# A two-layer perceiver on one Trainium2 core: the first layer's job order, its zero fills, one maximum over partitions and one projection's instruction order

## The chip, the cores and the metric

The kernel runs on one core of one Trainium2 chip. The metric is the device time of an execution in microseconds, given as the median of three runs. One further execution was profiled; the rows quoted below come from it. Engines are named as in the profile: PE (matrix multiply), DVE (vector), ACT (scalar, activation functions), POOL (general purpose), SP (issues most DMA transfers). Each engine takes its own instructions in order, and waits for others by semaphores.

## What is computed

The input x is 64 sequences of 32 tokens of width 256 (2048 tokens), beside a context of 64 x 257 x 256. Two layers follow, each with cross-attention, self-attention and a feed-forward block, all added to x after a layer norm. Everything is float32. Layer 0's blocks, cut to what matters here:

```
x = x + xattn(layernorm(x), ctx)             # 16 heads, causal: token l sees ctx[0..l]
x = x + attn(layernorm(x)) * gate ...        # 16 heads, position bias, tanh gate
# feed-forward with quantization to 16 bits ("qdq"):
def act_qdq(x):
    scale = maximum(max(abs(x)) / 32767, 1e-12)      # one maximum over the whole tensor
    return clip(round(x / scale), -32768, 32767) * scale
x = act_qdq(x); up = act_qdq(x @ deq(w_up).T); gate = act_qdq(x @ deq(w_gate).T)
sig = fixed_qdq_u16(sigmoid(gate)); gate = act_qdq(gate * sig); o = act_qdq(gate * up)
out = o @ deq(w_down).T
```

The three feed-forward weights are themselves rounded to 4 bits in blocks of 32 (`deq`).

## The kernel before

**Jobs.** Cross-attention and self-attention of layer 0 are cut into 16 jobs of 256 tokens (two tiles of 128): the order is x0 to x4, then a0, x5, a1, x6, a2, x7, then a3 to a7, where x is a cross-attention job and a a self-attention job. A loop over t = 0..15 (line 719 on) is a software pipeline written out by hand: in step t, job t is projected (values, keys, queries, L215 and L396), job t-1 gets its scores, maxima and exponentials (L255/L265, L282, L287, L697), job t-2 its normalization and block transposition (`weights_job`, L291 to L302) and its spread over four batch masks by ACT (L311), job t-3 its weighted sums (L322) and, at the end of its way, output projection (L347). A self-attention job that is done gives, in step t+4, the transposed input of the feed-forward block and its maximum (`f0_input`). Inside `tc.manual_schedule` the instructions of PE, DVE, ACT and POOL stand in the order in which they are written; SP's DMA issues are placed by the scheduler.

**Beside the jobs** the loop spreads other work: `dequantize` is a generator with 19 steps, one `next` each. For each of three weights: a DMA load, a maximum by block and its reciprocal (L508 to L511), multiplication and rounding (L513, L514), multiplication by the scale (L516), then three groups of four PE transposes with an ACT copy (L524, L527). `bias_heads` (L598) makes the position bias, `lines_matrices` (L423 to L455) small matrices for layer 1.

**Layer norm.** Statistics by DVE (L160, L161), rstd by two POOL instructions (L163, L164), the normalization xn by DVE (L368), then POOL adds a bias row to x (L414).

**Zeros.** `value_tiles` fills the tiles vz of the values with zeros once, by POOL (L481); the values are then written into every other block.

**The maximum over partitions** is `scale_of`/`scale_steps`: DVE reduces over the free axis (L537), POOL's `partition_all_reduce` over the partitions (L539). It is called for the quantized input ("x"), the gate, up, and two products. After step 1 of the loop there is one more such call on a constant, `warm` (L767).

**Gate projection.** 12 chunks of 1024 tokens by 128 features: four matmuls (L966), a copy by ACT (L971), a maximum by DVE (L359). In the same loop layer 1's weights are read chunk by chunk into two buffers (wck, L846) and OR-ed into `lost_bits` by DVE (L853). This loop is not in a hand-written order: the scheduler interleaves.

Of the kernel before, what the change touches and what calls it, by code (L numbers as in the profile page):

```python
# [11 lines left out]
F32 = mybir.dt.float32  # L12
# [4 lines left out]
ALU = mybir.AluOpType  # L17
AX = mybir.AxisListType
# [5 lines left out]
P = 128  # L24
# [42 lines left out]
def tile_perceiver(ctx: ExitStack, tc: tile.TileContext, d: dict, out: bass.AP):  # L67
    nc = tc.nc
# [26 lines left out]
    def load_x(n):  # L95
        nc.sync.dma_start(x[:, 2 * n : 2 * n + 2, :], x_view[:, 2 * n : 2 * n + 2, :])
# [10 lines left out]
    def load_rows(queue, a, b):  # L107
        queue.dma_start(
            rows[:, a:b].rearrange("p r e -> p (r e)"), d["rows"][a * D : b * D].partition_broadcast(P)
        )  # L110

    load_rows(nc.scalar, 0, 2)
    ident = const.tile([P, P], F32, tag="ident", name="ident")
    make_identity(nc, ident)
    eps = const.tile([P, 1], F32, tag="eps", name="eps")
    nc.gpsimd.memset(eps, EPS)
    mhalf = const.tile([P, 1], F32, tag="mhalf", name="mhalf")
    nc.gpsimd.memset(mhalf, -0.5)
    magic = const.tile([P, 1], F32, tag="magic", name="magic")
# [30 lines left out]
    def load_w(pool, name, n, kt=2):  # L150
        w = pool.tile([P, kt, n], F32, tag=name, name=name)
        nc.sync.dma_start(w, d[name].rearrange("(k p) n -> p k n", p=P))
        return w
# [49 lines left out]
    def row2(pool, name):  # L203

        r2 = pool.tile([P, 2, D], F32, tag=f"r_{name}", name="row2", bufs=1)
        nc.gpsimd.tensor_copy(r2, bc(row(name), 1, 2))
        return r2
# [265 lines left out]
            if i == 0:  # L473
                yield

    def value_tiles(pool, n):

        vzs = []
        for i in range(n):
            vz = pool.tile([P, 2, 8, 3, HD], F32, tag=f"vz{i}", name=f"vz{i}", bufs=1)  # L480
            nc.gpsimd.memset(vz, 0.0)  # L481
            vzs.append(vz)
        return cycle(vzs)

# [41 lines left out]
                    )  # L526
                nc.scalar.copy(flat[:, n0 * P : (n0 + 4) * P], pt)  # L527

    def scale_of(mx, tag, pre=None):
        *_, sr = scale_steps(mx, tag, pre)  # L530
        return sr

    def scale_steps(mx, tag, pre=None):


        m1 = small.tile([P, 1], F32, tag="m1", name="m1")
        nc.vector.tensor_reduce(m1, mx, AX.X, ALU.max)  # L537
        m2 = small.tile([P, 1], F32, tag="m2", name="m2")
        nc.gpsimd.partition_all_reduce(m2, m1, P, bass_isa.ReduceOp.max)  # L539
        yield  # L540
        s = small.tile([P, 1], F32, tag=f"s{tag}", name="s", bufs=1)
        if pre is not None:
            nc.vector.tensor_tensor(m2, m2, pre, ALU.mult)
        nc.vector.tensor_scalar(s, m2, 1.0 / QMAX, 1e-12, ALU.mult, ALU.max)
        r = small.tile([P, 1], F32, tag=f"r{tag}", name="r", bufs=1)
        nc.vector.reciprocal(r, s)
        if pre is not None:
            nc.vector.tensor_tensor(r, r, pre, ALU.mult)
        yield s, r


    with (
# [15 lines left out]
        x0_wv = load_w(wp, "x0_wv", D)  # L568
        x0_wk = load_w(wp, "x0_wk", D)
        x0_wq = load_w(wp, "x0_wq", D)  # L570
        load_x(1)
        load_c(1)
        x0_wo = load_w(wp, "x0_wo", D)
# [40 lines left out]
        def norm_job(w):  # L614
            w["xns"] = normalized(pool, w["n"], w["stats"])
            add_row2(w["n"], "a0_bo" if w["a"] else "x0_bo")

        def inputs_job(w):
            w["xT"] = pool.tile([P, 2, 2 * P], F32, tag="xT", name="xT", bufs=2)
            transposed(w["xns"], w["xT"])  # L620
# [15 lines left out]
        def keys_products(w):  # L636
            if w["a"]:
                w["pk"] = proj2(a0_wqkv, D, w["xT"])
            else:
                w["pk"] = proj2(x0_wk, 0, cTs[w["n"]])  # L640
                load_c(w["n"] + 3)

        def keys_apart(w):


            kb = w["kb"] = pool.tile([P, 2, 8, 4, L], F32, tag="kb", name="kb", bufs=2)
            bh = bias_of_head["a0_bk" if w["a"] else "x0_bk"]
            for m in range(2):
                for h in range(4):
                    nc.scalar.activation(  # L650
                        kb[:, m, :, h, :], w["pk"][:, m].rearrange("p (b l) -> p b l", l=L),
                        AF.Identity, bias=bh[:, m, h : h + 1], scale=h4[:, h : h + 1],
                    )
# [60 lines left out]


        with tc.manual_schedule(engines=hand_order):
            vzs = value_tiles(pool, 4)
            r2_x0 = row2(pool, "x0_bv")
            stats_of_job(jobs[0])
            norm_job(jobs[0])  # L720
            for t in range(NJ):
                proj, soft, turn, sums, done = (job(t - k) for k in range(5))
                f0 = done is not None and done["a"]
                if t < 2:
                    values_job(proj)
                    keys_products(proj)
                if turn:
                    weights_job(turn)
                if f0:
                    f0_input(done, 0)  # L730
                if job(t + 1):
                    stats_of_job(job(t + 1))
                if sums:
                    sums_job(sums)
                if f0:
                    f0_input(done, 1)
                if soft:
                    scores_job(soft)
                inputs_job(proj)
                if sums and proj["a"]:  # L740
                    out_job(sums)
                if t >= 2:
                    values_job(proj)
                if soft:
                    shift_job(soft)
                if turn:
                    spread_job(turn)
                if f0:
                    f0_input(done, 2)
                if soft:  # L750
                    exp_job(soft)
                if job(t + 1):
                    norm_job(job(t + 1))
                queries_job(proj)
                if t >= 2:
                    keys_products(proj)
                keys_apart(proj)
                gate_job(proj)
                if sums and not proj["a"]:
                    out_job(sums)  # L760
                if t == 0:
                    nc.vector.tensor_copy(mask8, bc(causal, 1, 8))
                elif t == 1:
                    r2_a0 = row2(pool, "a0_bv")

                    warm = small.tile([P, 1], F32, tag="m2", name="warm")
                    nc.gpsimd.partition_all_reduce(warm, eps, P, bass_isa.ReduceOp.max)  # L767
                elif t == 2:
                    bias_heads()
                    lines_of = lines_matrices(pool)  # L770
                elif t in (5, 6, 7):
                    next(lines_of, None)
                for _ in range(2 if 1 <= t <= 3 else 1):
                    next(dequantizing, None)
            for _ in dequantizing:
                pass


            j12, j13, j14, j15 = jobs[NJ - 4 :]
            weights_job(j14)  # L780
            sums_job(j13)
            scores_job(j15)
            shift_job(j15)
            spread_job(j14, 0, 2)
            exp_job(j15)
            spread_job(j14, 2, 4)
            out_job(j13)
            f0_input(j12, 0)
            weights_job(j15)
            f0_input(j12, 1)  # L790
            spread_job(j15, 0, 4, dve=(1, 3))
            sums_job(j14)
            f0_input(j12, 2)
            f0_input(j13, 0)
            sums_job(j15)
            f0_input(j13, 1)
            out_job(j14)
            f0_input(j13, 2)
            f0_input(j14, 0)
            out_job(j15)  # L800
            f0_input(j15, 0)
            f0_input(j14, 1)
            f0_input(j15, 1)
            f0_input(j14, 2)
            f0_input(j15, 2)


            sx, rx = scale_of(f0_mx, "x")
            for st in range(NST):
                xs = f0_xT[:, st].rearrange("p k n -> p (k n)")  # L810
                if st % 2 == 0:
                    nc.vector.tensor_scalar(xs, xs, rx, MAGIC, ALU.mult, ALU.add)
                else:
                    nc.scalar.activation(xs, xs, AF.Identity, bias=magic, scale=rx)
                nc.vector.tensor_scalar(xs, xs, MAGIC, sx, ALU.subtract, ALU.mult)
# [136 lines left out]
    with tc.tile_pool(name="f0", bufs=1, reuse_waits="tile") as pool:  # L952
# [19 lines left out]
            absmax(mx[:, c : c + 1], pm)  # L972

        mx = small.tile([P, NC], F32, tag="mx_g", name="mx", bufs=1)
        for c in range(NC):
            project(wgtT, g, c, mx)
            or_bits(weights_of(wck_pool, "wck", 2, *chunks[c]))
        checkp.close()
        sigp = ExitStack()
        sig_pool = sigp.enter_context(tc.tile_pool(name="sig", bufs=1, side="right", reuse_waits="tile"))  # L980
# [191 lines left out]
    with tc.tile_pool(name="x1", bufs=1, reuse_waits="tile") as pool:  # L1172
# [198 lines left out]
            load_ctx()  # L1371


        vzs = value_tiles(pool, 2)
        NP = 2 * H
        NP2 = NTILE // 2
        lns = []
# [597 lines left out]
```

## Time and profile before

| what | us |
|---|---|
| median of three runs (lowest, highest) | 1340.51 (1339.69, 1340.77) |
| the profiled execution's own time | 1338.12 |
| its span, first to last instruction | 1336.3 |
| layer 0's 16 jobs, first PE work to the maximum m (L537) | 8.28 to 256.48 |
| gate and up projections on PE begin (L966) | 262.76 |
| PE busy | 1227.4 |
| DVE busy | 908.6 |
| ACT busy | 719.7 |
| POOL busy | 159.9 |

A row of the timeline gives start, duration, engine, line, operation, and in brackets how long the engine was idle before it and what released it; "issue" stands for a wait for nothing that the profile shows. The chain of waits goes back from the last instruction, at each step to what released it. Rows of stretches give the busy time of every engine in a window.

### The profile page before, as it was taken

The numbers are of one execution on the slowest core, as the hardware profiler recorded it, in microseconds if no ns is written. First come the engines' busy times: TensorE is split into PE (matmuls) and PEld (weight loads), VectorE is DVE, ScalarE is ACT, GpSimd is POOL, SyncE is SP. The second block draws the span as 40 slices with busy tenths as digits, with TensorE's granted clock in tenths as the row PEclk, the third lists the DMA queues.
The fourth block names the chain that finished last, engine by engine and source line by source line (L and its number), as shares of the span: only waits on it lengthen the run. The fifth ranks groups of instructions, "written<-read, shape, count | busy, mean of one in ns | idle before, by whom it ended". The sixth has DMA issues, their size and how long they took to land.

```text
span 1336.3 us, 28421 instructions
## 1 busy us (share of the span) xinstructions
PE 1227.4 (92%) x11694; PEld 955.4 (72%) x11694; DVE 908.6 (68%) x1781; ACT 719.7 (54%) x1515; POOL 159.9 (12%) x423
## 2 busy tenths in 40 slices
PE   5799989599869999999999999999769999999998
PEld 4687878344558777777777777777557888888887
DVE  4788887866993488768787887777667363453633
ACT  3688878237693355667676766666535321131311
POOL 3111120100001012221212121211100000000000
PEclk9899999799989999999999999999879999999999
DMA  9200100230131342112111111110015100000000
GB/s 244 43 9 3 57 26 14 75 131 0 56 118 40 108 128 72 42 53 57 46 53 45 46 45 51 32 29 2 2 36 202 50 16 1 16 1 0 17 0 18
DMA packets 63127, 66.31 MB, mean 50 GB/s; under 512 B 21072, under 2 KB 52624, under 8 KB 62992
## 3 DMA queue, kind: packets, MB, share of 16 engines
q1 hardware_dynamic: 62416, 63.93, 16.1%
q8 instruction: 94, 1.54, 0.5%
q10 hardware_dynamic: 576, 0.50, 0.2%
q14 instruction: 41, 0.34, 0.1%
HBM read 57.53 MB, written 6.89 MB: 48 GB/s over the span
## 4 chain that ended last, share of the span: by engine, by line
PE 64%; DVE 23%; ACT 7%; issue 3%; DMA 2%; POOL 1%; SPq 0%; DVEq 0%; ACTq 0%; POOLq 0%
PE mm L1779 21%; PE mm L396 5%; PE mm L884 5%; PE mm L895 4%; PE pp L966 3%; PE mm L1274 3%; PE o L1112 3%; PE mm L215 3%; DVE nm L1236 2%; DVE mx L359 2%; PE s L1225 2%; PE o L1846 2%; DVE pe L1255 2%; PE o L1294 2%; PE o L347 1%
## 5 line engine op out<-in xcount | busy, mean ns | idle before, releaser
L1779 PE MATMUL mm<-hl,f_h 128*128 128x512 f32 x1024 | 232.9, 389 | 1.1 <-ACT sl L1824 1.1
L1779 PEld LDWEIGHTS mm<-hl,f_h 128*128 128x128 f32 x1024 | 192.2, 188 | 41.2 <-issue 1.4
L884 PE MATMUL mm<-ct,x_wk 128*128 128x257 f32 x512 | 132.2, 402 | 14.9 <-ACT kb L890 13.7
L1243 ACT ACTIVATE pe<-s,nm 128x257 f32<-128x257 f32 x256 | 118.2, 482 | 45.9 <-DVE nm L1236 21.1
L1837 ACT ACTIVATE g<-mm,cols 128x512 f32<-128x512 f32 x64 | 44.0, 688 | 164.8 <-PE mm L1779 163.6
L1785 DVE CAST hl<-g 128x512 fp32r<-128x512 f32 x64 | 27.3, 427 | 147.5 <-ACT g L1837 147.5
L895 PE MATMUL mm<-x_wv,ct 128*128 128x256 f32 x512 | 121.1, 379 | 0.4 <-ACT vb L929 0.4
L884 PEld LDWEIGHTS mm<-ct,x_wk 128*128 128x128 f32 x512 | 95.3, 196 | 36.6 <-ACT kb L890 15.7
L895 PEld LDWEIGHTS mm<-x_wv,ct 128*128 128x128 f32 x512 | 97.0, 190 | 14.6 <-ACT vb L929 0.8
L311 ACT ACTIVATE pb<-pt,masks 128x1024 f32<-128x1024 f32 x90 | 96.8, 1142 | 16.9 <-DVE pt L302 16.9
L1236 DVE TENSOR_REDUCE nm<-s 128x4 f32<-128x1028 f32 x64 | 78.2, 1222 | 15.1 <-PE s L1225 15.1
L890 ACT ACTIVATE kb<-mm,cols 128x257 f32<-128x257 f32 x128 | 57.7, 476 | 53.6 <-PE mm L884 49.8
L1263 POOL TENSOR_TENSOR px<-pe,rec 32x4 f32<-32x4 f32 x256 | 50.9, 199 | 276.5 <-DVE rec L1253 232.3
L1255 DVE TENSOR_SCALAR pe<-pe,rec 128x256 f32<-128x256 f32 x256 | 78.9, 371 | 5.4
L1274 PE MATMUL mm<-ident,pe 128*128 128x128 f32 x512 | 76.1, 283 | 7.0 <-DVE pe L1255 4.5
L1274 PEld LDWEIGHTS mm<-ident,pe 128*128 128x128 f32 x512 | 60.2, 142 | 23.6 <-issue 6.1
L414 POOL TENSOR_TENSOR x<-x,rows 128x512 f32<-128x512 f32 x32 | 45.3, 1415 | 133.9 <-DVE xn L368 130.7
L1243 ACT ACTIVATION_READ_ACCUMULATOR pe<-s,nm 128x1 f32 x256 | 54.9, 214 | 0.0
L911 DVE COPY vb<-mm 128x512 f32<-128x512 f32 x55 | 37.7, 685 | 23.9 <-PE mm L895 21.3
L384 ACT COPY xT<-mm 128x512 f32<-128x512 f32 x33 | 19.4, 587 | 61.9 <-PE mm L380 61.8
L1279 DVE COPY pT<-mm 128x512 f32<-128x512 f32 x64 | 44.0, 688 | 11.8 <-PE mm L1274 11.3
L1225 PE MATMUL s<-kb,qb 32*64 32x257 f32 x1024 | 44.4, 401 | 7.6 <-ACT pe L1243 4.2
(233 smaller groups left out, 2387.0 us busy)
## 6 DMA issues: line engine op xcount, KB each, us to landing
ct<-in_ctxT_dram SPq DMA_DIRECT2D x64, 257.0 KB, 2.8
raw<-in_f_h_dram SPq DMA_DIRECT2D x20, 512.0 KB, 4.2
wck<-in_f_h_dram SPq DMA_DIRECT2D x12, 512.0 KB, 3.7
raw<-in_f_w_dram SPq DMA_DIRECT2D x8, 512.0 KB, 3.8
dk<-kb SPq DMA_DIRECT2D x9, 257.0 KB, 3.1
kb<-dk SPq DMA_DIRECT2D x9, 257.0 KB, 2.7
dv<-vb SPq DMA_DIRECT2D x9, 256.0 KB, 3.1
vb<-dv SPq DMA_DIRECT2D x9, 256.0 KB, 2.7
```

The lines of the kernel that those rows point to most:

```text
L311: nc.scalar.activation(dst, src, AF.Copy, scale=scale)
L396: nc.tensor.matmul(pm[:, m * 2 * P : (m + 1) * 2 * P], lhsT=w[:, k, c0 + m * P : c0 + (m + 1) * P], rhs=src[:, k, :], start=(k == 0), stop ...
L884: nc.tensor.matmul(pm, lhsT=x1_wk[:, k, m * P : (m + 1) * P], rhs=ct[:, k, :], start=(k == 0), stop=(k == 1),)
L890: nc.scalar.activation(kb[:, m, :], pm, AF.Identity, bias=col("x1_bk", m))
L895: nc.tensor.matmul(pm[:, c * D : (c + 1) * D], lhsT=ct[:, k, c * P : (c + 1) * P], rhs=x1_wv[:, k, :], start=(k == 0), stop=(k == 1),)
L1225: nc.tensor.matmul(sc[64 * m : 64 * m + 64, r, :S], lhsT=qb[rs, m, b % 4].rearrange("p h l -> p (h l)"), rhs=kb[rs, m, :], start=True, sto ...
L1236: nc.vector.tensor_reduce(w["nm"], w["sc"][:, :, :S], AX.X, ALU.max, negate=True)
L1243: nc.scalar.activation(w["pe"][:, r, :], w["sc"][:, r, :S], AF.Exp, bias=w["nm"][:, r : r + 1], accum_out=w["sums"][:, r : r + 1],)
L1255: nc.vector.tensor_scalar(pe[:, r, :SK], pe[:, r, :SK], rec[:, r : r + 1], None, ALU.mult)
L1263: nc.gpsimd.tensor_tensor(x4[j * L : (j + 1) * L, q // 2, :, q % 2], pe[of, :, SK], rec[of], ALU.mult)
L1274: nc.tensor.transpose(pt[:, r * P : (r + 1) * P], pe[:, r, c * P : (c + 1) * P], ident)
L1779: nc.tensor.matmul(pm, lhsT=w[:, k, c0 : c0 + P], rhs=hl[k][:, part, :], start=(k == 0 and part == 0), stop=(k == kt - 1 and part == 1),)
```

## The change

- Job 0's transposes (`inputs_job`) are issued ahead of the loop, after its normalization, and the POOL copy of a bias row (`row2`) after those. The load of the first two bias rows moves from ACT's queue to SP's, behind the third weight.
- In step 1 the keys of job 1 are separated by heads (`keys_apart`) right after their products, ahead of the weights of other jobs.
- `bias_heads` moves from t = 2 to t = 3 (the steps of `lines_matrices` stay at t = 5, 6 and 7). The dequantizing generator is advanced twice at t = 4 only, before at t = 1, 2 and 3; the steps left over run after the loop.
- The zeros of layer 0's values are written by DVE, before by POOL.
- The call `warm` is gone.
- The maximum of the quantized input is spread on a diagonal (identity times m1), multiplied by a matrix of ones on PE, and reduced by DVE. The other four calls stay.
- The gate projection's loop stands in written order: the OR of chunk 0 first, then for each chunk the projection with its copy and maximum, the load two chunks ahead, the OR of the next chunk.

```
-    load_rows(nc.scalar, 0, 2)
...
+        load_rows(nc.sync, 0, 2)
...
-            nc.gpsimd.memset(vz, 0.0)
+            engine.memset(vz, 0.0)
...
         m2 = small.tile([P, 1], F32, tag="m2", name="m2")
-        nc.gpsimd.partition_all_reduce(m2, m1, P, bass_isa.ReduceOp.max)
+        if room is None:
+            nc.gpsimd.partition_all_reduce(m2, m1, P, bass_isa.ReduceOp.max)
+        else:
+            nc.vector.tensor_scalar(room, ident, m1, None, ALU.mult)
+            pm = bank("o")
+            nc.tensor.matmul(
+                pm[:, :P], lhsT=ones.to_broadcast([P, P]), rhs=room, start=True, stop=True
+            )
+            nc.vector.tensor_reduce(m2, pm[:, :P], AX.X, ALU.max)
...
-            vzs = value_tiles(pool, 4)
-            r2_x0 = row2(pool, "x0_bv")
+            vzs = value_tiles(pool, 4, nc.vector)
             stats_of_job(jobs[0])
             norm_job(jobs[0])
+            inputs_job(jobs[0])
+            r2_x0 = row2(pool, "x0_bv")
             for t in range(NJ):
...
                 if t < 2:
                     values_job(proj)
                     keys_products(proj)
+                if t == 1:
+                    keys_apart(proj)
...
-                inputs_job(proj)
+                if t > 0:
+                    inputs_job(proj)
...
-                keys_apart(proj)
+                if t != 1:
+                    keys_apart(proj)
...
-                    warm = small.tile([P, 1], F32, tag="m2", name="warm")
-                    nc.gpsimd.partition_all_reduce(warm, eps, P, bass_isa.ReduceOp.max)
-                elif t == 2:
+                elif t == 3:
                     bias_heads()
                     lines_of = lines_matrices(pool)
...
-                for _ in range(2 if 1 <= t <= 3 else 1):
+                for _ in range(2 if t == 4 else 1):
                     next(dequantizing, None)
...
-            sx, rx = scale_of(f0_mx, "x")
+            sx, rx = scale_of(f0_mx, "x", room=pool.tile([P, P], F32, tag="dg", name="dg"))
...
-        for c in range(NC):
-            project(wgtT, g, c, mx)
-            or_bits(weights_of(wck_pool, "wck", 2, *chunks[c]))
+        with tc.manual_schedule(engines=hand_order):
+            wck = [weights_of(wck_pool, "wck", 2, *chunks[c]) for c in range(2)]
+            or_bits(wck[0])
+            for c in range(NC):
+                project(wgtT, g, c, mx)
+                if c + 2 < NC:
+                    wck.append(weights_of(wck_pool, "wck", 2, *chunks[c + 2]))
+                if c + 1 < NC:
+                    or_bits(wck[c + 1])
```

More of the change, by code (lines that the diff above doesn't have):

```diff
@@ L116, in tile_perceiver @@
     nc.gpsimd.memset(eps, EPS)
+    ones = const.tile([P, 1], F32, tag="ones", name="ones")
+    nc.gpsimd.memset(ones, 1.0)
     mhalf = const.tile([P, 1], F32, tag="mhalf", name="mhalf")
@@ L474, in inverse_root, with value_tiles @@
                 yield
-    def value_tiles(pool, n):
+    def value_tiles(pool, n, engine):
         vzs = []
@@ L527, in dequantize, with scale_of, scale_steps @@
                 nc.scalar.copy(flat[:, n0 * P : (n0 + 4) * P], pt)
-    def scale_of(mx, tag, pre=None):
-        *_, sr = scale_steps(mx, tag, pre)
+    def scale_of(mx, tag, pre=None, room=None):
+        *_, sr = scale_steps(mx, tag, pre, room)
         return sr
-    def scale_steps(mx, tag, pre=None):
+    def scale_steps(mx, tag, pre=None, room=None):
         m1 = small.tile([P, 1], F32, tag="m1", name="m1")
@@ L1371, in tile_perceiver @@
             load_ctx()
-        vzs = value_tiles(pool, 2)
+        vzs = value_tiles(pool, 2, nc.gpsimd)
         NP = 2 * H
```

## The prediction

> **What bounds the kernel now.** I read the busy shares first, then the stretches of layer 0, then the chain of waits in the two places that the change touches. PE is busy 92% of the whole, so only a stretch in which PE idles can give time. The stretches (columns: stretch in us, its length, busy us of PE, weight loads, DVE, ACT and POOL, granted PE clock, DMA share, GB/s):
>
> ```profile
> 20.00:48.00 28.00, 16.66 (x237) 11.98 (x236) 21.44 (x33) 18.28 (x33) 5.67 (x8) 0.81 0.59 85
> 48.00:74.00 26.00, 25.92 (x424) 22.28 (x428) 18.15 (x28) 19.92 (x32) 4.35 (x6) 0.94 0.16 52
> 74.00:106.00 32.00, 29.22 (x558) 24.03 (x547) 30.33 (x54) 25.40 (x44) 4.49 (x7) 1.00 0.01 3
> 106.00:148.00 42.00, 41.83 (x635) 36.14 (x634) 33.71 (x60) 35.92 (x60) 8.29 (x13) 1.00 0.10 33
> 148.00:177.00 29.00, 24.03 (x397) 19.29 (x395) 25.73 (x41) 22.32 (x37) 6.06 (x8) 1.00 0.07 21
> ```
>
> PE idles 28.00-16.66 = 11.3 us in 20-48, 2.8 in 74-106 and 5.0 in 148-177, and is full elsewhere (57.63 of 58 from 177 to 235). In the last two DVE is nearly full (30.3 of 32, 25.7 of 29): the weight dequantization (s, w) is there. The chain shows what fills the first one (start, us, what):
>
> ```profile
> 39.91 2.60 issue
> 42.51 0.18 POOL rstd L163
> 42.77 0.75 POOL rstd L164
> 43.55 0.74 DVE xn L368 x2
> 44.28 0.39 DVE bias L598 x2
> 44.69 1.47 DVE bias L598 x2
> 46.17 1.77 DVE w L516
> 48.08 1.09 PE mm L524 x4
> 49.17 2.76 PE o L322 x64
> ```
>
> DVE stands still from 39.91 to 43.55 for an rstd whose input was there at 37.06; then bias and w run ahead of the four transposes for which PE waited. POOL's own rows tell why rstd was late (last bracket: idle before it):
>
> ```profile
> 34.40 0.57 POOL L767 PARTITION_ALL_REDUCE warm<-eps  x1 [5.76 <-issue]
> 42.51 0.18 POOL L163 TENSOR_TENSOR rstd<-mv,eps 128x2 f32<-128x2 f32 x1 [7.54 <-issue]
> 259.27 0.38 POOL L539 PARTITION_ALL_REDUCE m<-m  x1 [5.90 <-issue]
> ```
>
> Each change between an all-reduce and ordinary work costs POOL 5.8 to 7.5 us in which no instruction shows. At 256.65 the same thing stands on the chain, and behind it one instruction that the path does not need:
>
> ```profile
> 256.65 2.62 issue
> 259.27 0.39 POOL m L539
> ...
> 260.82 0.64 DVE lost_bits L853
> 261.46 0.41 issue
> 261.87 0.76 DVE f_xT L815
> 262.63 0.14 issue
> 262.76 43.05 PE pp L966 x96
> ```
>
> **How the stage was laid.** I laid the rows of the 16 jobs end to end, each engine in the order of its instruction listing, each start after its last producer, each duration from its row. For the order of before this puts mx of job 15 at 228.9 (trace: 232.8) and the maximum m at 251.5 (trace: 256.5). The missing 5.0 us are slow PE rows after idle time: L524 and L322 at 48 take 3.85 instead of 2.5 us (+1.4), L347 at 177 takes 3.51 instead of 1.73 (+1.8), L322 at 238 3.50 instead of 1.95 (+1.6). So the layout serves for differences, and the slow rows are added by hand.
>
> **First jobs.** The row load moves from ACT's queue to SP's behind x0_wq; row2 no longer stands ahead of rstd on POOL; job 0's transposes go ahead of its values. The listing also puts the fill of lost_bits (0.95) ahead of both rstd instructions, no longer between them. rstd starts at some 6 instead of 8.11, PE at 7.7 instead of 8.28, and queries follow keys without the wait for xT: 7.7+0.6+3.75+2.47+1.73 = 16.2 for their end, 1.4 us earlier. On SP the row load delays the issue of x, cT and x0_wo by its own 0.5 us; x (landed at 10.0, used at 12.68) and cT (10.2, 17.44) have that in hand. Keys apart for job 1 ahead of weights lets its scores end 2.4 us earlier in the layout. But the next thing on DVE is this row of the timeline:
>
> ```profile
> 26.68 1.75 DVE L508 TENSOR_REDUCE s<-w 128x48 f32<-128x1536 f32 x1
> ```
>
> Its load was issued at 19.16 and took 7.5 us: it lands at 26.66, in a queue that moves the same bytes either way. So this part is worth 0. If that load came earlier it would be worth up to 1.4; if x or cT came late, it would cost 0.5.
>
> **Zeros by DVE.** Four MEMSETs of 128x768. POOL's rows: 737 ns each. No DVE MEMSET is in the trace. [...] Cover: the weights land near 8 us. Path: 0.
>
> **No warm all-reduce.** xn waits no longer: 43.55-39.91 = 3.64 us of DVE at that point. Who waited behind xn: bias, w, the transposes, sums of job 0 on PE.
>
> **Other places for dequantization and bias.** The calls per t change from 1,2,2,2,1... to 1,1,1,1,2,1...; 17 of 19 steps run in the loop, two after it. Durations: s step 2.35, w by rs and rounding 2.65 (3.6 for the last weight), w by s 1.73, bias 1.9. At t=2 bias and w by s leave (3.6 us) and PE's transposes go to t=4. They come due at t=3, where PE had 25.92 busy of 26. The second weight's s moves from t=4 to 6, the third's from t=10 to 12, so its long step falls to t=13, again with an f0 input beside it; two groups of transposes fall behind the loop (0.9 us PE, 1.2 us ACT, in front of an ACT that waits for sm until 235.25). The layout, after minus before, for mx of jobs 2, 4, 6, 8, 11, 13, 15: -6.9, -8.6, -4.7, -4.8, -10.4, -7.2, -6.9; DVE's backlog returns part, PE's full stretches keep the rest. Taking only the all-reduce out gives -3.2; the places give the other 3.6. To this I add the 1.4 of slow rows at 48, since PE's gap before sums of job 0 shrinks from 9 to 1.9 us. The 1.8 at 177 I keep: in the new order a gap of 2.6 us stands at job 11's output. Stage: -6.9-1.4 = **-8.3** (ends: -4 if the backlog at t=12 to 14 is larger, -10.1 without the second slow row).
>
> **Maximum by PE.** Gone: 256.65 to 259.66, 3.0 us. Added: DVE 128x128 multiply, at the rate of L812 (1024 in 0.75) about 0.2; one PE matmul of 128x128, from L380 cold (four in 1.24) 0.3 plus about 0.1; DVE reduction of 128 from PSUM, 0.3 (512 take 0.69, 1024 take 1.22); three handovers. About 1.1. [...] The row decides: **-2.0** (ends -1 and -2.4). [...]
>
> **Gate projection in written order.** The first lost_bits leaves the stretch 260.82 to 261.87: **-1.1**. PE then runs 43 us full, as before; DVE alternates a maximum (1.22) and an OR (1.23) in a period of 3.43 us. Each OR waits for its load; behind it on DVE stands the next maximum, and four PSUM tiles behind that. wck loads took 3.7 us; with two buffers the period is (1.23+3.7+0.4)/2 = 2.7 us. Covered. The pair ACT copy, maximum at the end (305.84 to 308.12) stays.
>
> **Sum.** 8.3+2.0+1.1 = 11.4. The profiled execution is 1338.12 us (span 1336.3), 2.4 under the median 1340.51. Behind layer 0's gate everything follows on the chain (PE from 1018 on), nothing waits for a fixed time. 1338.12-11.4 = 1326.7; by the median **1329.1**.
>
> **Rivals.**
> 1. DVE's deferred work returns more: the stage keeps only the all-reduce's 3.2 and half of the rest; total 3.2+1.8+3.1 = 8 us: 1332.5. For it: 25.7 of 29 DVE in 148-177, now at t=12 to 14, nearer the end. 0.2.
> 2. All goes: also the slow row at 177 (1.8) and the first jobs' 1.4: 1325.9. For it: PE gap 2.6 against 3.4. 0.2.
> 3. [...] 0.04.
> 4. Slower: in-order DVE holds maxima behind late wck loads. It costs time once a load takes over 5.2 us (period 3.43) and outweighs all gains from 7.6 us on (period 4.6, ten chunks by 1.2 = 12): 1343 with loads of 8 us (period 4.8, +13.9), 1348 with 9. Against it: 3.7 median at 0.3 to 0.8 of DMA busy. 0.04.
>
> The likeliest case has 0.52. About 0.2% (2.7 us) is what a measurement here tells from no change. Faster by over 0.2%: 0.93 (all but rival 4 and some strays); within: 0.03; slower: 0.04. Range: rivals 1 to 2 with the bounds of the stage, 1324.8 to 1334.5.
>
> **What would show it.** xn of job 3 follows sm without a wait; L508's counterpart still starts near 26.7; PE idle in 20-48 falls to about 5; no POOL idle by issue before 250; from the maximum m to s about 1.1 us; first pp matmul 3 us after m's reduction, not 6.3; OR and maximum alternate with PE full. Wrong would make it: a long DVE-bound stretch at t=12 to 14 with more than 5 us of PE idle, gaps in pp, or first statistics after 6 us.

## The result, and the profile after

| | before | after |
|---|---|---|
| median of 8 runs each, the three quoted ahead among them (lowest, highest), us | 1339.72 (1336.65, 1340.77) | 1328.71 (1322.62, 1333.55) |
| ratio to before, 95% interval | | 0.9919 [0.9897, 0.9940] |
| the profiled execution, its span | 1338.12, 1336.3 | 1330.09, 1328.2 |
| mean granted PE clock (before: 42 later executions; after: these 8) | 0.971 | 0.974 |

The change saved 11.0 us by the medians, and 8.0 us between the two profiled executions. Both numbers are needed. Runs of one kernel differ by their clock: over 42 executions of the kernel before, an execution is 0.69 us shorter for every 0.001 of granted clock (correlation -0.82), so a 0.003 between two sets of runs goes with some 2 us, 2 of the 11.0 us here, and a step of 1 us can't be read from times. It can be read from places in the trace. I follow these (each "max" is the start of the row for scores of that job, DVE L282 before and L283 after):

| reached at, us | before | after | gain |
|---|---|---|---|
| score maximum of job 0 | 23.6 | 21.6 | 2.0 |
| block maxima of the first dequantized weight (L508, L509) | 26.68 | 27.80 | -1.1 |
| score maximum of job 2 | 53.9 | 47.4 | 6.5 |
| of job 8 | 134.6 | 128.6 | 6.0 |
| of job 11 | 177.1 | 165.1 | 12.0 |
| of job 15 | 232.8 | 224.1 | 8.7 |
| the maximum m (L537, L538) | 256.48 | 247.85 | 8.6 |
| first matmul of gate (L966, L979) | 262.76 | 251.68 | 11.1 |
| the reduction of the gate's maximum (L537, L538) | 308.14 | 298.51 | 9.6 |
| end of the span | 1336.3 | 1328.2 | 8.1 |

The stretches of layer 0 in the kernel after (stretch, its length, busy us of PE, weight loads, DVE, ACT and POOL, granted clock, DMA share, GB/s):

```profile
20.00:48.00 28.00, 21.74 (x375) 16.61 (x376) 22.85 (x31) 18.66 (x33) 5.92 (x8) 0.88 0.60 88
48.00:74.00 26.00, 23.98 (x402) 19.90 (x401) 21.90 (x35) 22.15 (x37) 4.95 (x7) 1.00 0.08 23
74.00:106.00 32.00, 31.74 (x439) 27.44 (x438) 25.00 (x51) 27.07 (x44) 5.59 (x8) 1.00 0.09 26
106.00:148.00 42.00, 39.38 (x656) 32.89 (x658) 37.06 (x58) 35.37 (x61) 7.64 (x12) 1.00 0.01 3
148.00:177.00 29.00, 28.83 (x495) 24.47 (x486) 25.71 (x44) 25.29 (x44) 5.26 (x8) 1.00 0.20 66
```

PE idles 6.3 us in the first stretch, before 11.3, and its clock in the first two is 0.88 and 1.00 where it was 0.81 and 0.94. The DVE-bound stretches at 74 and 148 are gone from there: PE is full. A little idle time is new at 48 to 74 and 106 to 148 (2.0 and 2.6 us), and one DVE-bound stretch comes later, at 169 to 194. The chain where the 3.6 us of waiting stood (start, us, what):

```profile
36.42 0.60 DVE vz L222
37.02 1.13 DVE sm L288
38.15 0.33 DVE xn L369
38.49 1.02 ACT sm L708
39.51 0.72 ACT qT L410 x2
40.23 3.65 ACT kb L661 x8
43.88 0.04 issue
43.93 0.45 PE sc L266 x16
```

xn follows sm at once, and the chain is now ACT's. Bias and w no longer stand in it. The way from the maximum to the first gate matmul, from the timeline:

```profile
247.85 0.16 DVE L538 TENSOR_REDUCE m<-f_mx 128x1 f32<-128x8 f32 x1
248.05 0.29 DVE L544 TENSOR_SCALAR dg<-ident,m 128x128 f32<-128x128 f32 x1
...
248.48 0.76 PE L546 MATMUL o<-dg,ones 128*128 128x128 f32 x2 [2.01 <-DVE dg L544]
...
249.28 0.29 DVE L549 TENSOR_REDUCE m<-o 128x1 f32<-128x128 f32 x1 [0.95 <-PE o L546]
249.61 0.15 DVE L554 TENSOR_SCALAR s<-m 128x1 f32<-128x1 f32 x1
...
250.00 0.75 DVE L825 TENSOR_SCALAR f_xT<-f_xT,r 128x1024 f32<-128x1024 f32 x1
...
251.68 10.58 PE L979 MATMUL pp<-f_xT,wgtT 128*128 128x512 f32 x17 [2.44 <-DVE f_xT L828]
```

From m to s it is 1.76 us, before 3.20 (256.48 to 259.68). From m to the first matmul it is 3.83, before 6.28. No OR stands between. The next all-reduce, on POOL:

```profile
298.81 0.38 POOL L541 PARTITION_ALL_REDUCE m<-m  x1 [54.07 <-DVE m L538]
```

It waits for its input alone: the row shows 54.07 us without other POOL work and no wait by issue, where there were 5.90 us at 259.27. The gate matmuls, though, take longer than before, by 1.45 us to the gate's maximum. The windows around their start, first before (they begin at 262.76), then after (251.68); the clock is the third number from the end:

```profile
262.70:266.70 4.00, 3.94 (x6) 1.82 (x7) 4.00 (x6) 0.00 (x0) 0.00 (x0) 0.59 0.57 175
266.70:270.70 4.00, 4.00 (x11) 1.79 (x10) 2.73 (x3) 1.01 (x1) 0.00 (x0) 1.00 0.64 221
```

```profile
250.00:254.00 4.00, 2.32 (x3) 1.18 (x4) 3.93 (x6) 2.38 (x2) 0.00 (x0) 0.50 0.83 267
254.00:258.00 4.00, 4.00 (x6) 1.55 (x5) 1.45 (x2) 0.00 (x0) 0.00 (x0) 0.52 0.35 120
258.00:262.00 4.00, 4.00 (x10) 1.71 (x9) 2.36 (x2) 1.14 (x2) 0.00 (x0) 1.00 0.03 11
```

A granted clock of 0.50 is called half rate, or half clock, here. If the half rate comes first in a window, a clock of 0.59 over 4 us is 3.3 us at half rate, so in before PE was at half rate until about 266.0, 3.2 us into the matmuls. In after 0.52 is 3.84 us, until 257.84 and 6.2 us in. L546 takes 0.76 us at a clock of 0.50 in after and 0.38 in e_early_keep, so 2.9 us more at half rate are 1.45 us of work.

### The profile page after: what moved, and what is told of

It is laid out like the page before. It is cut to its first block, busy times and chain, and to the rows that moved or that the text cites. A ratio compares the mean times of both kernels' runs of the same rounds, so it can differ in the third digit from the quotient of the medians.

```text
span 1328.2 us, 28424 instructions
## 1 busy us (share of the span) xinstructions
PE 1228.4 (92%) x11696; PEld 953.6 (72%) x11696; DVE 911.2 (69%) x1787; ACT 720.0 (54%) x1515; POOL 158.0 (12%) x418
## 4 chain that ended last, share of the span: by engine, by line
PE 62%; DVE 21%; ACT 11%; issue 2%; DMA 2%; POOL 0%; SPq 0%; DVEq 0%; ACTq 0%; POOLq 0%
PE mm L1798 21%; PE mm L897 5%; PE mm L397 5%; PE mm L908 4%; PE pp L979 3%; PE mm L1293 3%; PE o L1131 3%; DVE nm L1255 2%; PE mm L216 2%; ACT pb L312 2%; PE s L1244 2%; PE o L1865 2%; DVE mx L360 2%; DVE pe L1274 2%; ACT kb L661 2%
## 5 line engine op out<-in xcount | busy, mean ns | idle before, releaser
L903 ACT ACTIVATE kb<-mm,cols 128x257 f32<-128x257 f32 x128 | 57.8, 476 | 53.9 <-PE mm L897 49.9
L1262 ACT ACTIVATION_READ_ACCUMULATOR pe<-s,nm 128x1 f32 x256 | 54.8, 214 | 0.0
L1313 PEld LDWEIGHTS o<-pT,vb 128*32 128x32 f32 x2048 | 32.1, 110 | 25.7 <-issue 21.0
```

The lines of the kernel that those rows point to most:

```text
L903: nc.scalar.activation(kb[:, m, :], pm, AF.Identity, bias=col("x1_bk", m))
L1262: nc.scalar.activation(w["pe"][:, r, :], w["sc"][:, r, :S], AF.Exp, bias=w["nm"][:, r : r + 1], accum_out=w["sums"][:, r : r + 1],)
```

## The experiments

The theory: the time comes from the stage of jobs, because the all-reduce and the two DVE blocks behind it (bias, w) no longer keep PE waiting at 40 to 48, and from the way between m and the gate. The rivals: the first jobs' new order, or the written order of the gate, carries a good part; or the gain is only clock. Five kernels take one part each out of the changed kernel (u_), four put parts of it into the kernel before (b_), three go beyond the change (e_). "Time" is the median with its range and its ratio to before on the same chip; before itself has medians of 1336.24 to 1337.89 on the three chips used, so compare ratios (after: 0.9919). POOL's idle time by issue on either side of an all-reduce (5.76 and 7.54 us around `warm` in before) stands in the profile without a cause.

**The gate's loop left to the scheduler again** (rest of the change kept):

```
-        with tc.manual_schedule(engines=hand_order):
-            wck = [weights_of(...) for c in range(2)]
...
+        for c in range(NC):
+            project(wgtT, g, c, mx)
+            or_bits(weights_of(wck_pool, "wck", 2, *chunks[c]))
```

> The changed kernel with the gate projection's loop as before (the scheduler interleaves the ORs). Theory (the first OR stood on the path): an OR of 1.2 us lies again between the multiplication and the subtraction of the quantized input, the first pp matmul starts 1.1 us later after m's reduction than in the changed kernel (3.83 us there), whole time +1.1 us. Rival (the written order is worth nothing, or its waits cost): first matmul at 3.8 us still, time +0 or less.

m to s 1.76, m to the first matmul 3.83, the time from the first gate matmul to the gate's maximum 46.49 (after: 46.83), span 1326.8. Time 1329.31 (1327.80 to 1332.45), ratio 0.9938 [0.9914, 0.9961]. The OR did not come back between L825 and L828; the scheduler puts it behind. The written order is worth nothing here. By the times this kernel is 0.2% above after, with overlapping intervals: so much they leave open.

**The maximum by POOL again**, gate in written order:

```
-            sx, rx = scale_of(f0_mx, "x", room=pool.tile([P, P], F32, tag="dg", name="dg"))
+            sx, rx = scale_of(f0_mx, "x")
```

> The changed kernel with POOL's all-reduce for the quantized input's maximum. [...]

m to s 3.03 (before: 3.20), m to the first matmul 6.11, against 1.76 and 3.83. The timeline of this kernel:

```profile
253.99 0.38 POOL L541 PARTITION_ALL_REDUCE m<-m  x1 [5.73 <-issue]
...
255.46 1.22 DVE L866 TENSOR_TENSOR lost_bits<-lost_bits,wck 128x1024 int32<-128x1024 int32 x1
256.59 1.41 DVE L828 TENSOR_SCALAR f_xT<-f_xT,s 128x1024 f32<-128x1024 f32 x2
...
257.48 2.90 PE L979 MATMUL pp<-f_xT,wgtT 128*128 128x512 f32 x3 [7.49 <-DVE f_xT L828]
```

The wait by issue and the OR are both back, though the gate's loop is in written order: the OR's place ahead of L828 goes with the POOL maximum, not with that loop. Time 1331.83 (1327.25 to 1337.40), ratio 0.9952 [0.9936, 0.9968]. Its m lies at 251.37, 3.5 us later than in after, from something that this edit does not touch: the clock in 124 to 128 and 196 to 200 is 0.58 and 0.57, in after 1.00 in both. I count only the 2.3 us behind m for this part. In after 1.2 of them are lost again at the gate, where it is 45.62 us from the first matmul to the maximum here and 46.83 there; 1.1 are left.

**The all-reduce `warm` back in step 1:**

```
                     r2_a0 = row2(pool, "a0_bv")
+                    warm = small.tile([P, 1], F32, tag="m2", name="warm")
+                    nc.gpsimd.partition_all_reduce(warm, eps, P, bass_isa.ReduceOp.max)
```

> The changed kernel with the warm all-reduce after step 1 again. Theory: POOL stands still 5.8 us before and 7.5 us behind it, xn of job 3 waits some 3.4 us on DVE, m comes 3.2 us later, whole time +3.2 us. Rival (PE and ACT are the bound there, the wait is hidden): xn waits, m moves by less than 1 us.

POOL's rows in it:

```profile
32.51 0.38 POOL L782 PARTITION_ALL_REDUCE warm<-eps  x1 [5.73 <-issue]
40.00 0.19 POOL L164 TENSOR_TENSOR rstd<-mv,eps 128x2 f32<-128x2 f32 x1 [7.12 <-issue]
```

xn waits 3.87 us for that rstd (the idle time of DVE before it). From job 3 to job 8 every score maximum is 1.8 to 2.3 us later than in after (63.0, 130.4 against 61.2, 128.6), at job 15 3.1, at m 4.4; what is added from 124 on has half clock in it (0.64 in 124 to 128). Time 1331.77 (1328.81 to 1335.00), ratio 0.9951 [0.9935, 0.9967].

**The old places of dequantization and bias:**

```
-                elif t == 3:
+                elif t == 2:
                     bias_heads()
...
-                for _ in range(2 if t == 4 else 1):
+                for _ in range(2 if 1 <= t <= 3 else 1):
                     next(dequantizing, None)
```

> The changed kernel with dequantization and bias at their old places in the loop. Theory (the old places made PE wait for DVE while DVE had room later): PE idles again some 3 us more in 20 to 48, m comes 3.6 to 5 us later, whole time +3.6 to +5 us. Rival (DVE's work is only moved, and comes due again at t=12 to 14): m moves by less than 2 us.

Job 2's score maximum moves from 47.4 to 51.9, job 15's from 224.1 to 230.7 (6.6 us), m from 247.85 to 255.63 (7.8). PE idles 13.1 us in 20 to 48, and the stretches at 74 and 148 are DVE's again (PE 29.21 of 32, 24.03 of 29). Time 1335.64 (1326.25 to 1337.13), ratio 0.9981 [0.9968, 0.9993]: without the new places hardly anything of the change is left.

**The first jobs, the row load and the zeros as before:**

```
-            inputs_job(jobs[0])
-            r2_x0 = row2(pool, "x0_bv")
             for t in range(NJ):
...
-                if t == 1:
-                    keys_apart(proj)
...
-            vzs = value_tiles(pool, 4, nc.vector)
+            vzs = value_tiles(pool, 4, nc.gpsimd)
```

> The changed kernel with the first jobs as before: zeros by POOL, row load on ACT's queue, row2 ahead of the statistics, job 0's transposes inside the loop, keys of job 1 apart at their old place. Theory (the load of the first feed-forward weight sets when DVE goes on, near 27 us): queries of job 0 end about 1.4 us later, but the s reduction starts at the same time within 0.3 us, m and the whole time move by less than 0.5 us. Rival (the early part is on the path): m and the time +1.4 to +2.4 us.

DVE waits for the load here too, only less long:

```profile
27.33 1.75 DVE L510 TENSOR_REDUCE s<-w 128x48 f32<-128x1536 f32 x1 [1.72 <-DMA w<-in_f_gt_dram]
```

Score maxima of jobs 0 to 8: 22.5, 34.8, 47.4, 61.4 ... 128.7, against 21.6, 35.2, 47.4, 61.2 ... 128.6 in after. So these parts give nothing until job 8. From job 9 on it is 1.6 us late; a stretch of half clock falls at 124 (0.60 in 124 to 128). The same stretch is in u_pool_max and e_keep_busy, whose edits lie behind the jobs, so it needs no cause in the first jobs. Span 1327.6 (after: 1328.2), time 1331.20 (1327.88 to 1334.42), ratio 0.9957 [0.9941, 0.9973]. By the times it is 0.4% slower than after and the intervals just fail to meet, while the span says equal; where those 5 us would lie no profile shows, so for the whole time the worth of these parts stays open.

**The load that ends the first jobs, issued earlier** (an edit beyond the change: the first feed-forward weight's load goes ahead of the load of a0_wqkv on SP):

```
+        dequantizing = dequantize(pool)
+        next(dequantizing)
         a0_wqkv = load_w(wp, "a0_wqkv", 3 * D)
...
-                for _ in range(2 if t == 4 else 1):
+                for _ in range(2 if t == 4 else 0 if t == 0 else 1):
```

> The changed kernel with the load of the first feed-forward weight issued ahead of the self-attention weights. Theory (that load is what DVE waits for, 3.1 us at 24.7): the s reduction starts right after xn of job 2, near 24.7 us, and the first jobs' gain is kept: m comes 1.5 to 3 us earlier, whole time -1.5 to -3 us. Rival (ACT's chain pb, exp, kb is the bound from there on): the wait vanishes, m moves by less than 0.7 us.

The row of the block maxima, first in after, then here:

```profile
27.80 1.75 DVE L509 TENSOR_REDUCE s<-w 128x48 f32<-128x1536 f32 x1 [3.11 <-DMA w<-in_f_gt_dram]
```

```profile
24.88 1.75 DVE L509 TENSOR_REDUCE s<-w 128x48 f32<-128x1536 f32 x1
```

DVE waits 3.11 us for the load in after and not at all here; every later score maximum up to job 15 is 2.8 to 3.0 us earlier, m 2.9. This experiment shows the anchor of the first part: what was gained ahead of it (2.0 us at job 0) was lost in this wait. The clock in 20 to 48 is 1.00 (after: 0.88) and no half clock shows before 227. Time 1326.15 (1320.11 to 1331.31), ratio 0.9924 [0.9894, 0.9953], so the times don't tell it from after; its profile is of the fastest of its six runs (span 1318.2).

**Parts put into the kernel before.** b_no_warm only drops the all-reduce, b_places only has the new places, b_both has the two, b_pe_max only the maximum by PE. The edits are the ones above, the other way round.

> The kernel before with only the warm all-reduce taken out. Theory: xn of job 3 no longer waits 3.65 us, m comes 3.2 us earlier, and the whole time -3.2 us. [...]

> The kernel before with only dequantization and bias at their new places. Theory: m comes 3.6 us earlier by the layout, 1.4 us more if the slow PE rows at 48 vanish: whole time -3.6 to -5 us. Rival (with the warm all-reduce in place the two waits of DVE overlap): less than -2 us.

> The kernel before with two edits: no warm all-reduce, and dequantization and bias at their new places. Theory (each alone leaves the other's wait standing, together they free DVE): mx of job 15 comes 7 to 9 us earlier than before's 232.8 (the two alone gave 1.7 and 1.5), m to s stays near 3.1, whole time -7 to -9 us. Rival (the first jobs' new order is what carries the rest): no more than the sum of the two alone, -3 to -4 us.

> The kernel before with only the quantized input's maximum by PE. Theory (the place of the first OR follows the engine of the maximum, not the loop's written order): m to first pp matmul 3.83 us, not 6.28; whole time -2.4 us at most, -1.2 where PE's clock then stays at half for one window more. Rival (the written order is needed to move the OR): 4.9 us from m to the first pp matmul.

| score maximum of | job 2 | job 8 | job 15, us | gain at 8, at 15 | time (range) | ratio |
|---|---|---|---|---|---|---|
| before | 53.9 | 134.6 | 232.8 | | | 1 |
| b_no_warm | 51.8 | 132.5 | 231.1 | 2.1, 1.7 | 1334.59 (1329.11 to 1336.82) | 0.9979 [0.9966, 0.9992] |
| b_places | 52.7 | 132.6 | 231.3 | 2.0, 1.5 | 1337.34 (1332.41 to 1341.34) | 0.9997 [0.9981, 1.0013] |
| b_both | 47.6 | 128.9 | 225.9 | 5.8, 6.9 | 1330.99 (1328.23 to 1334.12) | 0.9954 [0.9936, 0.9972] |
| b_pe_max | 54.8 | 135.5 | 232.0 | -0.9, 0.7 | 1337.21 (1334.63 to 1341.21) | 1.0009 [0.9995, 1.0023] |

At job 15 it is 1.7 and 1.5 alone and 6.9 together. Some of that is the place of the half clock: b_places has a second stretch of it (0.57 in 200 to 204), which takes some 1.7 us, b_both has one, at 124, and b_no_warm has one, at 177, as before has. None of these has touched job 8 yet, which follows job 7 after 13.4 us in all four. There it is 2.1 and 2.0 alone and 5.8 together: the parts do not add, by 1.7 us. (At m the gains are 0.5, 1.4 and 6.9.) b_both at job 8 is also within 0.3 us of after, without the new order of the first jobs. The chains tell why the parts don't add. First b_no_warm, then b_places:

```profile
39.01 1.13 DVE sm L287
40.14 0.64 DVE xn L368 x2
...
41.20 1.47 DVE bias L598 x2
42.67 0.01 issue
42.68 1.77 DVE w L516
44.45 0.14 issue
44.59 1.09 PE mm L524 x4
45.67 3.57 PE o L322 x64
```

```profile
37.99 1.14 DVE sm L287
39.13 3.16 issue
42.30 0.19 POOL rstd L163
...
43.34 0.73 DVE xn L368 x2
44.08 1.68 DVE w L513
45.76 0.02 issue
45.78 1.91 DVE w L514
47.69 1.14 DVE sums L291
```

Without the all-reduce xn is on time, but bias and w still keep PE from its next work until 44.59, and PE then does its sums at half rate (3.57 for 64 matmuls, 1.88 at full rate). With the new places bias and w are gone, but xn waits 3.2 us for rstd, and w of the step behind it comes on top. Two obstacles stand one behind the other at the same place: whoever removes one finds the other. The first jobs' parts matter only while the all-reduce is there: u_warm and b_places differ ahead of job 8 in these parts alone. With them POOL comes to rstd at 40.00, without them at 42.30, and job 8 follows at 130.4 and 132.6.

b_pe_max: m to s 1.76, m to the first matmul 3.84, with no OR between, which settles that the maximum by PE alone moves the OR away. 2.4 us are gained at that place, but the matmuls take 1.06 us longer (46.44 against 45.38), and the time is that of before. This kernel also shows that a stretch of half clock in the jobs can come and go without an edit to them. Its edit lies behind the jobs, and yet the slow output projection at 177 is gone, after the same idle time; first before, then b_pe_max:

```profile
176.93 3.51 PE L347 MATMUL o<-a_wo,oT 128*128 128x256 f32 x8 [2.87 <-DVE oT L336]
```

```profile
177.88 1.99 PE L349 MATMUL o<-a_wo,oT 128*128 128x256 f32 x8 [2.87 <-DVE oT L338]
```

**PE kept at work ahead of the gate.** The four matmuls that are added have no reader.

```
+            def keep_busy():
+                pw = bank("mm")
+                for _ in range(2):
+                    nc.tensor.matmul(pw, lhsT=ident, rhs=wgtT[:, 0, 0:512], start=True, stop=True)
+            keep_busy()
             sx, rx = scale_of(f0_mx, "x", room=...)
+            keep_busy()
```

> The changed kernel with four matmuls whose result nobody reads (128x128 by 128x512): two behind the last transposes of layer 0's jobs, two behind the maximum's matmul. Theory (PE's idle time ahead of the gate projection brings the half clock, which lasted some 6 us into it): PE gaps there shrink below 1 us, the gate and up stretch from first pp matmul to the gate's maximum falls from 46.8 to 45.3 us or less, time -1.5. [...]

m to s 1.47, m to the first matmul 3.54, the matmuls to the gate's maximum 43.78, which is 3.05 less than after. The clock is 0.74 in 248 to 252 and 1.00 in 252 to 260, so the gate matmuls start at full rate (254.07); in after half rate lasts 13.65 us, from 244.16 to 257.81. The gate's maximum is at 297.85, 0.7 ahead of after, since m came 2.7 us later in this profile (clock 0.60 in 124 to 128, 0.64 in 196 to 200). Time 1328.56 (1325.99 to 1330.59), ratio 0.9931 [0.9912, 0.9950], the same as after.

**Both together**, the early load and the added matmuls:

> The changed kernel with the early load of the first feed-forward weight and the four matmuls nobody reads. Theory: both gains add, m at 245 as with the early load alone, first pp matmul to the gate's maximum 45.3 us or less, whole time -3 to -4 us against the changed kernel. Rival: the load's gain alone, -1.5 to -3 us.

Timeline and windows of this kernel:

```profile
243.37 2.65 PE L824 MATMUL mm<-wgtT,ident 128*128 128x512 f32 x4
...
245.86 0.38 PE L546 MATMUL o<-dg,ones 128*128 128x128 f32 x2
...
246.08 1.88 PE L824 MATMUL mm<-wgtT,ident 128*128 128x512 f32 x4
...
248.68 11.82 PE L988 MATMUL pp<-f_xT,wgtT 128*128 128x512 f32 x27 [0.72 <-DVE f_xT L837]
```

```profile
248.00:252.00 4.00, 3.33 (x8) 1.63 (x9) 3.96 (x6) 1.45 (x2) 0.00 (x0) 1.00 0.63 222
252.00:256.00 4.00, 4.00 (x10) 1.71 (x9) 2.80 (x3) 1.20 (x2) 0.00 (x0) 1.00 0.38 131
```

The clock is 1.00 from the first gate matmul on, L546 takes 0.38 (after: 0.76 at half rate), and the gate's maximum is at 292.46, 6.05 us ahead of after. Time 1323.64 (1321.24 to 1326.44), ratio 0.9897 [0.9877, 0.9916]: the best median of all. Its interval still touches that of after (at 0.9897), so the times alone don't prove it faster than after; in the profiles two places speak for it (m 2.9 us earlier, gate matmuls 3.05 shorter), and its span is 1321.8 (after: 1328.2).

## Why the prediction was right, and where it was not

**The time.** 1328.71 was measured, 1329.1 forecast. Much of this closeness is luck: the sum was 11.4 us on the profiled execution, which shows 8.0, and terms of the sum missed in both directions. Up to the first gate matmul the profiles agree with it (11.1 gained). Then 1.45 us go at the gate, and 1.5 us behind it (1028.16 from the gate's maximum to the end in before, 1029.69 in after, with the same instructions; over the profiles of the other kernels it lies anywhere from 1024.2 to 1030.0). The medians gained more than the profiles, with a mean clock of 0.974 against 0.971; why is not shown.

**First jobs and zeros: 0. Right as far as job 8; open for the whole time (u_first).** The anchor was right: the load, not the engines, sets when DVE starts on the weight. It landed at 27.8 instead of 26.66, since it took 8.58 us from its issue instead of 7.5, so the part even had a small cost there, and u_first shows equal progress up to job 8. "If that load came earlier it would be worth up to 1.4" was too small: in e_early_load it is 2.9 at m. The DVE zeros took 698 ns each, on POOL 735, and three in a row 2.31 us (0.95 to 3.25), on POOL 2.11; the statistics start at 4.47 instead of 3.95. The cover held, and job 0's maximum came 2.0 us earlier.

**The stage of jobs: -8.3, measured -8.6 at m. The sum came out by luck; its split was wrong.** The step was "Taking only the all-reduce out gives -3.2; the places give the other 3.6", plus 1.4. Taken out of before alone, the all-reduce gives 2.1 at job 8 and the places 2.0; undone from after, they cost 1.9 and 4.0. The layout had bias and w behind xn, so it knew of the second obstacle, but it laid the rows at one rate. In b_no_warm PE starts on L524 3.5 us earlier than in before (44.59 against 48.08), and then takes 7.15 us instead of 5.79 up to job 3's transposes (L380); the 64 matmuls of L322 there take 3.57 us instead of 2.76. That leaves 2.1. The slow rows go once bias and w no longer stand ahead of PE: L322 takes 1.96 in b_places. With both parts the 1.4 did come: jobs 4, 6, 8 and 11 are 1.3 to 1.9 us further ahead than in the layout.

Two more terms missed, and cancelled. "The 1.8 at 177 I keep" failed: the output projection behind DVE's late stretch (194.69 in after) took 1.99 us, not 3.51. b_pe_max has it at 1.99 too, without any edit to the jobs (and takes 14.55 us from the score maximum of job 11 to that of job 12, before 16.23). So some 1.7 us of the gain go with the place of the half clock, and nothing shows them to be the change's work. And the layout took too little for the last two jobs: between the score maxima of jobs 13 and 15 it lost 0.3 us, while after takes 29.24 us and before 27.43, a loss of 1.8. b_both takes 29.24 and u_places 27.42, so the loss goes with the new places. That is the rest: 6.9 + 1.4 + 1.7 - 1.5 = 8.5, measured 8.65 at job 15. The late DVE stretch itself came as described: the chain is DVE's from 169.16 to 194.33, and PE idles 3.8 us in 177 to 226.

**Maximum by PE: -2.0, measured -1.44 from m to s.** The term that was mis-sized is "one PE matmul of 128x128 ... 0.3 plus about 0.1". It took 0.76: PE had idled for 2.01 us, and the granted clock was 0.50; in e_early_keep, with PE kept at work, it took 0.38. The two DVE rows were 0.29 each, forecast at 0.2 and 0.3. POOL's row of 0.38 us is not the price of the way by POOL: in u_pool_max, with 5.73 us of idle time by issue ahead of that row, m to s took 3.03.

**The gate's written order: -1.1, measured 0.** The OR did leave the path, but the maximum by PE moved it: it is away in u_gate_order and b_pe_max, and back in u_pool_max. Undoing the written order changes neither m to the first matmul (3.83) nor, by more than 0.4 us, the stretch of the matmuls (46.49 against 46.83). The step failed by crediting the OR's new place to the edit nearest to it. Together the two terms were 3.1 and gave 2.45 up to the first matmul, all of it by the maximum on PE.

**Not foreseen: 1.45 us back at the gate matmuls.** "PE then runs 43 us full, as before" was wrong: it ran 44.50. The wait ahead of the gate was cut from 7.66 to 2.44 us, but PE idled 2.01 us ahead of L546 too, and the half clock ended 6.2 us into the matmuls, in before 3.2. In b_pe_max 1.06 of 2.4 us go back at the matmuls too; the 1.4 left do not show in its times (1.0009 [0.9995, 1.0023]), and its part behind the gate's maximum is the slowest of all profiles (1030.0). e_keep_busy and e_early_keep show that it is the clock: with the idle time filled (0.72 us left) it is 1.00 where the gate matmuls start, and the same matmuls take 3.05 us less. How much comes back is not fixed: u_first and e_early_load have the same edit and the same idle time ahead of the gate (2.44 us), and they took 45.57 and 45.25 us to the gate's maximum, against 46.83 in after.

**The rivals.** The first (DVE's deferred work returns more) did happen in the last two jobs, with 1.5 us, but not in the sum at m. The second's part at 177 did happen, by chance, without its total. No new wait of POOL came up at the gate's maximum: the all-reduce at 298.81 waits for its input alone. The fourth is refuted by the gate stretch: before, the ORs waited there eight times for wck, 6.4 us in all; after, none waits for a load.

## What to carry to other kernels

Ask of every removed wait what stands right behind it: here the all-reduce and the bias work were two obstacles at one place, worth 2.1 and 2.0 us alone and 5.8 together at job 8, so a trial of each by itself would have valued both too low. To say which edit moves an instruction, compare the listings of each edit alone; the whole change only tells that it moved. Where PE idles ahead of a dense stretch, read the granted clock of its first microseconds (here half rate for 6.2 us, behind 2.44 us of idle time), and try whether filling the gap with matmuls that nobody reads pays; here it took 3.05 us off the stretch, and its time alone did not show it (0.9931 against 0.9919).

## What was not expected of the hardware

The half clock comes in pieces of one length. The stretches of half rate in the clock records of before and after last 3.41, 6.83 or 13.65 us, multiples of 3.41, but for the one in which each execution ends. Of the 2.4 us that b_pe_max gains ahead of the gate, 1.06 went back at the gate matmuls. The place of a piece changes between kernels whose jobs are the same: those at 124 and 196 show in u_pool_max and e_keep_busy (from job 8's score maximum to job 9's 11.94 and 11.95 us, from job 13's to job 14's 16.03 and 16.01), and not in after or u_gate_order (10.49 and 10.50, then 14.56 and 14.55). What sets the place is not shown.
